# A relational graph convolution: 172 spare columns at the end of a ring of sums, and copies one part behind the matrix engine

## The chip, the core and the metric

The kernel runs on one core of a Trainium2 chip. A core has a matrix engine (TensorE, PE in the profile; its weight loads are PEld), a vector engine (VectorE, DVE), an activation engine (ScalarE, ACT), GpSimd (POOL), a synchronisation engine that issues transfers (SyncE, SP), and 16 DMA engines that all transfers share. Each engine runs its own instructions in order and waits for others by semaphores. SBUF is the on-chip memory with 128 partitions; PSUM holds what TensorE writes. The metric is the device time of one launch in microseconds (us), the median of several runs.

## What is computed

Two layers of a relational graph convolution with 12,500 nodes, 128 features, 200,000 edges sorted by destination, and 10 relations; then a residual and a layer norm. An edge's relation is the argmax of ten of its attributes.

```
def _rgcn_layer(x, src, dst, edge_type, w_rel, root, bias):
    seg = dst * NUM_REL + edge_type
    sums = segment_sum(x[src], seg)
    cnt  = segment_sum(ones, seg)
    mean = (sums / maximum(cnt, 1)[:, None]).reshape(N, NUM_REL, -1)
    return einsum('nrd,rdo->no', mean, w_rel) + x @ root + bias

h   = relu(_rgcn_layer(x, src, dst, edge_type, w_rel1, root1, b1))
out = layernorm(x + _rgcn_layer(h, src, dst, edge_type, w_rel2, root2, b2))
```

## The kernel before

**Tiles and parts.** The edges are cut into 1,563 tiles of 128. `STEP` is 8: on average a tile moves on by 8 destination nodes. `OFF` is 80: a tile's first node lies within 80 of where the average puts it (the kernel clamps it, and falls back to a slow path if an input breaks the bound). Four tiles make a *part* (`QB`); layer 1 is a loop over parts `p`.

**What a part does** (`layer_1`). POOL gathers the rows of the tile's sources into a buffer `g` (`gathered`, L801), one DMA per tile: first from `x`, later from `XH`, which holds rows of `x` beside rows of the first layer's result for nodes that are finished. DVE makes a 0/1 table `oh` that places each edge at (relation, node in the window) (`ones`, L813), and ACT scales it by 1 / count (`weighted`, L807). TensorE multiplies both into `zp` in PSUM (L1038). DVE adds `zp` to the sums `cc` (`sum_into`, L837). From tile 177 on, each tile gives two products, one for layer 1's sums (`cc[:, 0]`) and one for the share of layer 2's sums that can already be known (`cc[:, 1]`).

The order is written out by hand: in the loop's turn `p`, tables are made for part p + 2, scaled for p + 1, rows gathered and multiplied for p, and sums added for p - 2. A list of due times (`todo`) holds the rest; an entry due at `t + n * u` runs `n` parts after its block was finished. `g` has six buffers of eight rows, of which four (`NEAR`), one part each, serve the tiles from 177 on; `zp` has four banks, two per part.

**The ring.** `cc` holds, for each of two layers and ten relations, `RW` columns of nodes: 1,024 (`RN`) and a few behind. Node n has column n mod 1,024, so the ring comes round every 1,024 nodes, that is every 128 tiles; I call that a *lap*. A tile writes 12 columns (`WN`) from its first node's column, which is read at run time from a row `b_r` (DMA at L1049, loaded into DVE's registers at L822, a row per 128 tiles). A tile just in front of a lap's end may so write beyond column 1,023. When the first block of a lap is finished, `folded` adds those columns to the beginning of the ring and clears them:

```
s, e = cc[:, ls, :, :w], cc[:, ls, :, RN:RN + w]
nc.vector.tensor_tensor(s, s, e, op=ALU.add)      # L785
nc.vector.memset(e, 0.0)                          # L786
```

Since the column is known only at run time, each addition declares the lowest and highest column that its tile could have (`offsets`), and the waits are made from that. A tile whose possible nodes lie on both sides of a multiple of 1,024 declares columns 0 to 1,023.

**Blocks.** A *block* is 256 nodes (128 near the end; 52 in all). When all tiles that can reach it are summed, `finish(k, t)` runs: `projected` multiplies its sums by ten relation matrices and the root (L794, L796); ACT adds the bias (`rows_copied`, L717); TensorE transposes the result (`rows_out`, L918), ACT copies it (`rows_kept`, L925), and SP stores it to `XH` (L670) and, not transposed, to `hT` (L930). `projected_rows` multiplies the result by layer 2's ten matrices in three groups per 128 nodes: a product into the one PSUM tile `yb` (L906), ACT's copy to `ys` (L907), SP's store to the table `YD`. `cleared` (ACT, L767) sets the block's columns to zero for the next lap. Gathers may use a block's rows in `XH` from seven parts (`READY`) after it was finished, for blocks 3 to 43.

**Layer 2** goes over the edges again: those that could not be taken in layer 1 are brought together in lists on the chip (`brought_together`, `listed`), and their rows gathered from `YD`. It works in the same memory as the ring (`every` is `cc` as one row per partition): the sums `acc2` begin at column `FIRST`, lists and tables lie below.

Of the kernel before, what the change touches and what calls it, by code (L numbers as in the profile page):

```python
# [39 lines left out]
CT = 128  # L40
YB = 512
RN = 2 * YB
RW = RN + WMAX
RT = 11
REACH = 560
SIGMAS = 4.25
# [10 lines left out]
LOW = 1 << 13  # L57
TOPN = (1 << 14) - 1
OFF = 80
W = 128  # L60
GT = 125
EPS = 1e-5
# [4 lines left out]
def rgcn_resnorm_kernel(ctx: ExitStack, tc: tile.TileContext, x, src, dst, attr, w_rel1, root1, b1,  # L67
# [289 lines left out]
    def places():  # L357
        off = keep.tile([NCH, CT], F32, name="off")
        early(0, nc.vector.tensor_tensor(off, b_i, even, op=ALU.subtract))
        b_f = keep.tile([NCH, CT], F32, name="b_f")  # L360
        lows = keep.tile([NCH, CT], F32, name="lows")
        early(0, nc.vector.memset(lows, 0.0))
        for size in (BN, P):
            for k in range(NBLK - 1):
                if done_after(k) < NT and starts[k + 1] - starts[k] == size:
                    early(0, nc.vector.scalar_tensor_tensor(lows, even, STEP * done_after(k) - 0.5, lows,
                                                            op0=ALU.is_gt, op1=ALU.add))
            if size == BN:
                early(0, nc.vector.tensor_scalar(lows, lows, float(BN // P), None, op0=ALU.mult))
        early(0, nc.vector.tensor_scalar(lows, lows, float(P), None, op0=ALU.mult))  # L370
        early(0, nc.vector.tensor_scalar(b_f, off, float(OFF), -float(OFF), op0=ALU.min, op1=ALU.max))
        early(0, nc.vector.tensor_tensor(b_f, b_f, even, op=ALU.add))
        early(0, nc.vector.tensor_tensor(b_f, b_f, lows, op=ALU.max))
        early(0, nc.vector.tensor_tensor(lows, b_i, lows, op=ALU.is_lt))
        early(0, nc.vector.tensor_scalar(b_i, b_f, 0.0, float(N - 1), op0=ALU.max, op1=ALU.min))
        early(0, nc.vector.tensor_scalar(b_r, b_i, RN - 1, None, op0=ALU.bitwise_and))
        nc.vector.tensor_tensor(off, off, off, op=ALU.mult)
        nc.vector.tensor_scalar(off, off, float(OFF) ** 2 + 0.5, None, op0=ALU.is_gt)
        nc.vector.tensor_tensor(off, off, lows, op=ALU.max)
        worst = keep.tile([NCH, 1], F32, name="worst")  # L380
        nc.vector.tensor_reduce(worst, off, axis=AX.X, op=ALU.max)
        nc.vector.tensor_tensor(fl[:NCH], fl[:NCH], worst, op=ALU.max)
# [397 lines left out]
    def folded(ls, k, w):  # L780

        if block(k)[0] % RN or not k:
            return
# [33 lines left out]
    def offsets(row, t0, n, limits, ring=True):  # L817

        lims = [limits(t0 + j) for j in range(n)]
        if ring:  # L820
            lims = [(lo % RN, hi % RN) if lo // RN == hi // RN else (0, RN - 1) for lo, hi in lims]
        vals = nc.values_load_multi_w_load_instructions(  # L822
            row, engines=[DVE], min_val=min(a for a, _ in lims), max_val=max(b for _, b in lims),
            skip_runtime_bounds_check_because="clamped to these nodes on the chip")[1]
        return [nc.s_assert_within(v, a, b, skip_runtime_bounds_check_because="clamped to these nodes on the chip")
                for v, (a, b) in zip(vals, lims)]
# [50 lines left out]
    def layer_1():  # L877
# [6 lines left out]
        def finish(k, t):  # L884
# [4 lines left out]
                xbs[k] = rows_in(k)  # L889
                fTs[k] = features_in(k, 0, xbs[k])  # L890
            u = QB if t < NT else 0
            folded(ALL, k, WN)
            o = block(k)[0] % RN
            po = [projected(k, 0, cc[:, 0, :, o:o + block(k)[1]], rsb[0], fTs[k])]
            both = has_sums(k)
# [5 lines left out]
                fin_a[k] = shifted(a, k, 0)  # L901

            def projected_rows(b, h, r):
                a, ys = fin_a[k], next_of("ys", staged)
                m = min(HB, NREL - r) * C
                nc.tensor.matmul(yb[:h, :m], a[:, b * P:b * P + h], wsb[1][:, r:r + m // C, :], start=True, stop=True)  # L906
                nc.scalar.activation(ys[:h, :m], yb[:h, :m], AF.Copy)  # L907
# [25 lines left out]
            todo.at(t + u, rows_copied)  # L933
            if k <= K1:
                todo.at(t + 2 * u, rows_out)
                todo.at(t + 2 * u, rows_kept)
            else:
                hbs.pop(k, None)
            todo.at(t + 2 * u, features_kept)
            for j, (b, h, r) in enumerate(groups):  # L940
                todo.at(t + (2 + j if k <= K1 else 1 + j) * u, lambda _, b=b, h=h, r=r: projected_rows(b, h, r))
# [12 lines left out]
            if k + 1 < NBLK - 1:  # L954
                def fetch(t):
                    xbs[k + 1] = rows_in(k + 1)

                def turn(t):
                    n0, n, subs = block(k + 1)
                    pt = ps_f.tile([P, YB], F32, name="pf")  # L960
                    for i, h in subs:
                        nc.tensor.transpose(pt[:, i * P:i * P + h], xbs[k + 1][:h, i, :], ident[:h, :h])
# [10 lines left out]
                todo.at(t + (w + 1) * u, turned_kept)  # L973

        fin_a = {}
        yb = ps_z.tile([P, YB], F32, name="yb")
# [151 lines left out]
    def brought_together(ready, first):  # L1128
# [23 lines left out]
        assert at <= FIRST  # L1152
        yield 1
        nc.vector.memset(below, 1.0)
        nc.vector.tensor_scalar(below[:, :P], columns, place, None, op0=ALU.is_ge)
# [125 lines left out]
    def listed(c):  # L1281
# [48 lines left out]
        w = comp.tile([P, P], F32, name="wb")  # L1330
# [19 lines left out]
    def layer_2():  # L1350
# [396 lines left out]
```

## Time and profile before

| | us |
|---|---|
| median of 3 runs | 3,130.71 (3,126.43 to 3,132.64) |
| profiled execution, whole | 3,124.18 |
| profiled execution, first to last instruction (span) | 3,122.4 |
| POOL busy | 2,296.9 (74%) |
| PE busy | 2,227.4 (71%) |
| DVE busy | 1,631.5 (52%) |
| ACT busy | 1,114.4 (36%) |
| first gather of layer 1 starts / last one | 4.08 / 2,006.72 |
| last gather of layer 2 starts | 3,104.05 |

How to read the rows that follow. A row of the timeline has the start in us, the duration, the engine, the line, the operation with what it writes and reads, the count, and in brackets how long the engine had been idle before it and what ended that. A row of the groups has the count, then the busy time in us, the mean duration in ns, and the idle time before, with what ended most of it. `PE zp L1038` as a releaser is TensorE's product of a part. "issue" means that the profile shows nothing that was waited for. A queue's own instructions (`SPq`, `ACTq`) issue transfers.

### The profile page before, as it was taken

What the parts mean: (1) busy time and instruction counts of PE and PEld (TensorE: products, weight loads), DVE (VectorE), ACT (ScalarE), POOL (GpSimd) and SP (SyncE); (2) the same over time, 40 slices, a digit from 0 to 9 for tenths busy, and PEclk for the clock granted to TensorE, in tenths of its full rate; (3) what the DMA queues carried; (4) which work ended last, traced back from release to release, by engine and by line L of the source; (5) the groups of instructions that cost most, each with busy time, mean ns of one, the idle gap of its engine ahead of it and who ended that gap; (6) DMA issues with size and microseconds to landing.
All of it is one profiled execution on the core that took longest, in us unless ns stands there. A gap on an engine that the chain in (4) does not pass through costs nothing. (4 is left out here: it accounts for less than half of the span.)

```text
span 3122.4 us, 42050 instructions
## 1 busy us (share of the span) xinstructions
PE 2227.4 (71%) x11120; PEld 1813.5 (58%) x11120; DVE 1631.5 (52%) x5055; ACT 1114.4 (36%) x3222; POOL 2296.9 (74%) x2437
## 2 busy tenths in 40 slices
PE   2877776868687877778787777754777777767554
PEld 1656655656575666666666566644666666656543
DVE  6664665847474746464656564368642323333332
ACT  3644442534343444444444444331222212221221
POOL 7777776767777777777776777667777777777775
PEclk7789897979888889888898989855777777776555
DMA  6756656656667666666666666542355555554222
GB/s 175 228 159 189 220 170 192 197 184 204 201 188 219 183 219 186 207 197 198 202 192 204 183 188 191 160 109 61 109 161 165 168 158 159 164 166 131 78 69 56
DMA packets 377357, 529.96 MB, mean 170 GB/s; under 512 B 56782, under 2 KB 284501, under 8 KB 377110
## 3 DMA queue, kind: packets, MB, share of 16 engines
q0 software_dynamic: 99776, 249.91, 28.6%
q1 hardware_dynamic: 249111, 264.44, 26.5%
q10 hardware_dynamic: 28223, 12.82, 1.5%
q8 instruction: 93, 1.52, 0.2%
q14 instruction: 154, 1.26, 0.1%
HBM read 373.17 MB, written 160.19 MB: 171 GB/s over the span
## 5 line engine op out<-in xcount | busy, mean ns | idle before, releaser
L801 POOL DMA_INDIRECT g<-XH,idxE x1386 | 1310.8, 946 | 471.7 <-issue 199.8
L1038 PE MATMUL zp<-oh,g 128*128 128x120 f32 x5898 | 958.2, 312 | 455.9 <-DMA g<-XH,idxE 183.8
L1038 PEld LDWEIGHTS zp<-oh,g 128*128 128x128 f32 x5898 | 859.3, 218 | 676.0 <-issue 182.2
L837 DVE TENSOR_TENSOR cc<-cc,zp 128x240 f32 (+1 forms) x1563 | 607.2, 389 | 780.0 <-PE zp L1038 476.5
L801 POOL DMA_INDIRECT g<-YD,idxB x685 | 647.6, 945 | 208.8 <-issue 135.6
L807 ACT ACTIVATE oh<-oh,wE 128x120 f32<-128x120 f32 (+1 forms) x1740 | 517.8, 374 | 86.0 <-DVE oh L813 66.6
L1540 PE MATMUL zy<-oh,g 128*128 128x12 f32 (+22 forms) x1170 | 240.8, 329 | 232.7 <-DMA g<-YD,idxB 145.1
L1540 PEld LDWEIGHTS zy<-oh,g 128*128 128x128 f32 x1170 | 221.8, 264 | 265.5 <-DMA g<-YD,idxB 120.7
L907 ACT ACTIVATE ys<-yb 128x512 f32<-128x512 f32 (+2 forms) x294 | 154.0, 524 | 617.4 <-PE yb L906 609.9
L906 PE MATMUL yb<-w,a 128*128 128x512 f32 (+1 forms) x576 | 306.1, 619 | 1.4 <-ACT ys L907 1.4
L794 PE MATMUL alone<-cc,w 128*128 128x256 f32 (+2 forms) x920 | 295.4, 498 | 1.8 <-DVE cc L1462 1.8
L794 PEld LDWEIGHTS alone<-cc,w 128*128 128x128 f32 x920 | 237.4, 273 | 45.8 <-DVE cc L1462 2.0
L813 DVE TENSOR_TENSOR oh<-bank,keyE 128x480 f32<-128x480 f32 x391 | 253.4, 648 | 0.0
L794 PE MATMUL pf<-cc,w 128*128 128x256 f32 (+2 forms) x1040 | 241.3, 391 | 5.8 <-DVE cc L785 3.1
L767 ACT ACTIVATE cc<-zero 128x1280 f32<-128x1280 f32 (+2 forms) x184 | 224.7, 1225 | 10.1 <-DVE cc L837 4.1
L794 PEld LDWEIGHTS pf<-cc,w 128*128 128x128 f32 x1040 | 202.9, 209 | 36.1 <-DVE cc L837 4.8
L801 POOL DMA_INDIRECT g<-YD,idxE x177 | 169.5, 957 | 71.5 <-issue 37.8
L801 POOL DMA_INDIRECT g<-in_x_dram,idxE x177 | 167.4, 946 | 55.6 <-issue 34.1
L807 ACT ACTIVATE oh<-oh,wB 128x16 f32<-128x16 f32 (+27 forms) x685 | 159.6, 305 | 128.5 <-DVE oh L813 62.4
L751 ACT ACTIVATE rstd<-mv,eps 128x2 f32<-128x2 f32 (+2 forms) x52 | 15.3, 295 | 519.9 <-DVE mv L749 519.8
L1540 PE MATMUL zq<-oh,g 128*128 128x16 f32 (+24 forms) x554 | 107.3, 314 | 100.1 <-DMA g<-YD,idxB 92.9
L1540 PEld LDWEIGHTS zq<-oh,g 128*128 128x128 f32 x554 | 97.3, 242 | 114.4 <-DMA g<-YD,idxB 76.3
(251 smaller groups left out, 1584.6 us busy)
## 6 DMA issues: line engine op xcount, KB each, us to landing
SD<-cc SPq DMA_DIRECT2D x41, 1280.0 KB
cc<-SD SPq DMA_DIRECT2D x41, 1280.0 KB
YD<-ys SPq DMA_DIRECT2D x194, 256.0 KB
m<-in_edge_attr_dram SPq DMA_DIRECT2D x48, 672.0 KB
g<-XH,idxE POOLq DMA_INDIRECT x1386
YD<-ys SPq DMA_DIRECT2D x97, 128.0 KB
XH<-hb SPq DMA_DIRECT2D x44, 256.0 KB
g<-YD,idxB POOLq DMA_INDIRECT x685
```

The costliest lines, as they stand in the source:

```text
L751: nc.scalar.activation(rstd[:p, s], mv[:p, s, 1], AF.Sqrt, bias=eps[:p])
L767: nc.scalar.activation(cc[:, l, h * H:(h + 1) * H, o:o + n], zero[:, None, :n].to_broadcast([P, H, n]), AF.Copy)
L794: nc.tensor.matmul(po[:, :n], wsb[l][:, r, :], sums[:, r], start=(r == 0), stop=(w is None and r == NREL - 1))
L801: nc.gpsimd.indirect_dma_start(out=g[:, j * C:(j + n) * C], out_offset=None, in_=table, in_offset=bass.IndirectOffsetOnAxis(ap=idx, axis=0))
L807: nc.scalar.activation(s, s, AF.Copy, scale=w)
L813: nc.vector.tensor_tensor(o.rearrange("p (t m) -> p t m", m=m), cols[:, None, :m].to_broadcast([P, n, m]), keys[:, :, None].to_broadcast([ ...
L837: nc.vector.tensor_tensor(s, s, z, op=ALU.add)
L906: nc.tensor.matmul(yb[:h, :m], a[:, b * P:b * P + h], wsb[1][:, r:r + m // C, :], start=True, stop=True)
L907: nc.scalar.activation(ys[:h, :m], yb[:h, :m], AF.Copy)
L1038: nc.tensor.matmul(zp[:, o + l * KW:o + (l + 1) * KW], g[:, (slot[j] + l) * C:(slot[j] + l + 1) * C], oh[:, j * KW:(j + 1) * KW], start=Tr ...
L1540: nc.tensor.matmul(zp[:, j * w:(j + 1) * w], g[:, at * C:(at + 1) * C], oh[:, j * w:(j + 1) * w], start=True, stop=True)
```

## The change

The change has three pieces.

1. *More columns.* `EDGE` = 2 x 80 + 12 = 172 columns stand behind the ring's 1,024 where 120 stood. A tile's column is now counted from the lap in which its *earliest* possible node lies, so a tile in front of a lap's end goes on into the columns behind 1,023 and never wraps by itself; `b_r` is worked out so, and `offsets` declares the same range, which no longer spans the ring. `folded` adds and clears 172 columns instead of 12.
2. *Copies one part later.* `projected_rows` no longer copies its own product. It puts the copy and store (`projected_kept`) aside, and the next group's call, one part later, does them first. `rows_kept` is due at `t + 3 * u` instead of `t + 2 * u`.
3. *Room.* The longer ring takes 4,160 bytes more per partition. Layer 2's tiles `h` and `v` move into the ring's memory below `FIRST`, and `wb` uses `tri`'s buffer.

```
+EDGE = 2 * OFF + WN
+RW = RN + EDGE
...
-        early(0, nc.vector.tensor_scalar(b_r, b_i, RN - 1, None, op0=ALU.bitwise_and))
+        early(0, nc.vector.tensor_scalar(b_r, even, -float(OFF), 0.0, op0=ALU.add, op1=ALU.max))
+        lap_of = keep.tile([NCH, CT], I32, name="lap_of")
+        early(0, nc.vector.tensor_scalar(lap_of, b_r, RN - 1, None, op0=ALU.bitwise_and))
+        early(0, nc.vector.tensor_tensor(b_r, lap_of, b_r, op=ALU.subtract))
+        early(0, nc.vector.tensor_tensor(b_r, b_i, b_r, op=ALU.add))
...
-            lims = [(lo % RN, hi % RN) if lo // RN == hi // RN else (0, RN - 1) for lo, hi in lims]
+            laps = [max(0, (t0 + j) * STEP - OFF) // RN * RN for j in range(n)]
+            lims = [(lo - a, hi - a) for (lo, hi), a in zip(lims, laps)]
...
-            folded(ALL, k, WN)
+            folded(ALL, k, EDGE)
...
             def projected_rows(b, h, r):
+                kept_rows()
                 m = min(HB, NREL - r) * C
-                nc.tensor.matmul(yb[:h, :m], a[:, b * P:b * P + h], wsb[1][:, r:r + m // C, :], start=True, stop=True)
+                nc.tensor.matmul(yb[:h, :m], fin_a[k][:, b * P:b * P + h], wsb[1][:, r:r + m // C, :], start=True, stop=True)
+                unkept.append(lambda: projected_kept(b, h, r))
+
+            def projected_kept(b, h, r):
+                ys = next_of("ys", staged)
+                m = min(HB, NREL - r) * C
                 nc.scalar.activation(ys[:h, :m], yb[:h, :m], AF.Copy)
...
-                todo.at(t + 2 * u, rows_kept)
+                todo.at(t + 3 * u, rows_kept)
...
+            todo.at(t + (i + 1) * u, kept_rows)
...
+        def kept_rows(_=None):
+            if unkept:
+                unkept.pop()()
...
-        vs = [comp.tile([P, 2, C], F32, name=f"v{i}") for i in range(1)]
+        vs = [every[:, FIRST - 4 * BN:FIRST - 3 * BN].rearrange("p (t c) -> p t c", c=C)]
...
-        hs = [comp.tile([P, BN], F32, name=f"h{i}") for i in range(3)]
+        hs = [every[:, FIRST - (i + 1) * BN:FIRST - i * BN] for i in range(3)]
```

What this does to the order of instructions, at three places. First DVE's order with its waits, at the first addition in front of the lap at node 5,120 (L837 before, L844 after; `ISA` rows work out the address in registers; L490 and L495 end an argmax, L813 and L818 make a table). Before:

```order
L490 TENSOR_SCALAR ty<-bank 128x32 [waits DVE_49]
L837 ISA
L837 TENSOR_TENSOR cc<-cc,zp_404 128x20x12 [waits DMAHW0_49,DMAHW2_49,PE_49,Activation_49]
L837 ISA
L837 TENSOR_TENSOR cc<-cc,zp_404 128x20x12 [waits DVE_49]
L813 TENSOR_TENSOR oh_93<-bank,keyE 128x480
L837 ISA
L837 TENSOR_TENSOR cc<-cc,zp_401 128x20x12 [waits PE_49,Activation_49]
```

After:

```order
L495 TENSOR_SCALAR ty<-bank 128x32 [waits DVE_49]
L844 ISA
L844 TENSOR_TENSOR cc<-cc,zp_409 128x20x12 [waits PE_49]
L844 ISA
L844 TENSOR_TENSOR cc<-cc,zp_409 128x20x12 [waits DVE_49]
L818 TENSOR_TENSOR oh_93<-bank,keyE 128x480 [waits Activation_49]
L844 ISA
L844 TENSOR_TENSOR cc<-cc,zp_406 128x20x12 [waits DVE_49,PE_49]
```

The instructions stand as they stood; the additions no longer wait for ACT or for transfers, and the table's own wait for ACT (for the scaling of the buffer's last contents) is now written down where it was implied before.

Second DVE's order at a fold, that of the lap that begins at node 5,120 (`cc<-cc` is the addition, the `MEMSET` behind it the clearing; the sizes are partitions x 20 rows x columns). Before:

```order
L837 TENSOR_TENSOR cc<-cc,zp_402 128x20x12
L785 TENSOR_TENSOR cc<-cc 128x20x12
L786 MEMSET cc 128x20x12
L813 TENSOR_TENSOR oh_92<-bank,keyE 128x480
L837 ISA
```

After:

```order
L844 TENSOR_TENSOR cc<-cc,zp_407 128x20x12
L790 TENSOR_TENSOR cc<-cc 128x20x172
L791 MEMSET cc 128x20x172
L818 TENSOR_TENSOR oh_92<-bank,keyE 128x480
L844 ISA
```

Nothing moved; the two instructions have 3,440 elements per partition instead of 240.

Third ACT's order from the finishing of a block on (`hb<-pf` copies the transposed rows, `ys<-yb` a projected group, `cc<-zero` clears, `oh<-oh` scales one part's four tables). Before:

```order
L807 ACTIVATE oh_97<-oh_97,wE 128x120 x4
L925 ACTIVATE hb_6439<-pf 128x2x128
L907 ACTIVATE ys_99<-yb 128x512
L767 ACTIVATE cc<-zero 128x5x256
L807 ACTIVATE oh_98<-oh_98,wE 128x120 x4
L907 ACTIVATE ys_100<-yb 128x512
L767 ACTIVATE cc<-zero 128x5x256
L807 ACTIVATE oh_92<-oh_92,wE 128x120 x4
```

After:

```order
L812 ACTIVATE oh_97<-oh_97,wE 128x120 x4
L772 ACTIVATE cc<-zero 128x5x256
L812 ACTIVATE oh_98<-oh_98,wE 128x120 x4
L937 ACTIVATE hb_6445<-pf 128x2x128
L919 ACTIVATE ys_99<-yb 128x512
L772 ACTIVATE cc<-zero 128x5x256
L812 ACTIVATE oh_92<-oh_92,wE 128x120 x4
```

The copies of rows and of the first group stand behind the next part's scalings, and the first clearing in front of them; of the number of instructions nothing changed here.

More of the change, by code (lines that the diff above doesn't have):

```diff
@@ L42 @@
 RN = 2 * YB
-RW = RN + WMAX
 RT = 11
@@ L820, in offsets @@
         if ring:
-            lims = [(lo % RN, hi % RN) if lo // RN == hi // RN else (0, RN - 1) for lo, hi in lims]
+            laps = [max(0, (t0 + j) * STEP - OFF) // RN * RN for j in range(n)]
+            lims = [(lo - a, hi - a) for (lo, hi), a in zip(lims, laps)]
+            assert all(hi + WN <= RW for _, hi in lims)
         vals = nc.values_load_multi_w_load_instructions(
@@ L903, in projected_rows @@
             def projected_rows(b, h, r):
-                a, ys = fin_a[k], next_of("ys", staged)
+                kept_rows()
                 m = min(HB, NREL - r) * C
-                nc.tensor.matmul(yb[:h, :m], a[:, b * P:b * P + h], wsb[1][:, r:r + m // C, :], start=True, stop=True)
+                nc.tensor.matmul(yb[:h, :m], fin_a[k][:, b * P:b * P + h], wsb[1][:, r:r + m // C, :], start=True, stop=True)
[3 more added lines that the diff above has]
+                m = min(HB, NREL - r) * C
                 nc.scalar.activation(ys[:h, :m], yb[:h, :m], AF.Copy)
@@ L940, in finish @@
             for j, (b, h, r) in enumerate(groups):
-                todo.at(t + (2 + j if k <= K1 else 1 + j) * u, lambda _, b=b, h=h, r=r: projected_rows(b, h, r))
+                i = 2 + j if k <= K1 else 1 + j
+                todo.at(t + i * u, lambda _, b=b, h=h, r=r: projected_rows(b, h, r))
+            todo.at(t + (i + 1) * u, kept_rows)
             if reused:
@@ L973, in finish @@
                 todo.at(t + (w + 1) * u, turned_kept)
+        unkept = []
+        def kept_rows(_=None):
+            if unkept:
+                unkept.pop()()
         fin_a = {}
@@ L1151, in brought_together @@
         tri = comp.tile([P, P], F32, name="tri")
-        assert at <= FIRST
+        assert at <= FIRST - 4 * BN
         yield 1
@@ L1329, in listed @@
         nc.vector.tensor_scalar(li[:p], li[:p], P - 1, None, op0=ALU.bitwise_and)
-        w = comp.tile([P, P], F32, name="wb")
+        w = comp.tile([P, P], F32, name="tri")
         nc.vector.tensor_scalar(w[:p], li[:p], 1.0, None, op0=ALU.max)
```

## The prediction

> **What bounds the kernel now.** I read the page's groups by engine first. POOL is the busiest engine (74%), and everything it does is issuing row gathers:
>
> ```profile
> L801 POOL DMA_INDIRECT g<-XH,idxE x1386 | 1310.8, 946 | 471.7 <-issue 199.8
> L801 POOL DMA_INDIRECT g<-YD,idxB x685 | 647.6, 945 | 208.8 <-issue 135.6
> L801 POOL DMA_INDIRECT g<-YD,idxE x177 | 169.5, 957 | 71.5 <-issue 37.8
> L801 POOL DMA_INDIRECT g<-in_x_dram,idxE x177 | 167.4, 946 | 55.6 <-issue 34.1
> ```
>
> That is 2,425 gathers, 946 ns busy each. The idle time before one is usually 0.30 us, whatever is named as its releaser, as the timeline of POOL below shows. So a gather that nothing holds up comes 1.25 us after the one before it, in both layers: 2,425 x 1.25 = 3,031 us of the 3,122.4. The kernel is a queue of gathers, and a change is worth what it takes from, or adds to, the delays of that queue. Next, POOL's rows around a place where the ring of sums comes round, and those that mark off layer 1 (177 + 1,386 = 1,563 gathers):
>
> ```profile
> 4.08 1.11 POOL L801 DMA_INDIRECT g<-in_x_dram,idxE  x1 [1.92 <-DVE lane L339]
> ...
> 691.14 0.95 POOL L801 DMA_INDIRECT g<-XH,idxE  x1 [0.30 <-issue]
> 696.41 0.94 POOL L801 DMA_INDIRECT g<-XH,idxE  x1 [4.33 <-PE zp L1038]
> ...
> 708.56 0.94 POOL L801 DMA_INDIRECT g<-XH,idxE  x1 [4.44 <-PE zp L1038]
> ...
> 2006.72 0.94 POOL L801 DMA_INDIRECT g<-XH,idxE  x1 [2.09 <-PE zp L1038]
> 2016.54 0.94 POOL L801 DMA_INDIRECT g<-YD,idxE  x1 [8.88 <-PE zp L1038]
> ...
> 2039.24 0.94 POOL L801 DMA_INDIRECT g<-YD,idxE  x1 [9.29 <-DMA h<-hT]
> ```
>
> From the first gather to the 1,563rd are 2,002.64 us; 1,562 steps of 1.25 would be 1,952.5. So layer 1 loses 50.1 us, nearly all of it like the rows at 696.41 and 708.56: POOL waits until TensorE has read a gather buffer. Why TensorE is late there is in DVE's and ACT's timelines at the next such place:
>
> ```profile
> 829.23 0.84 DVE L837 TENSOR_TENSOR cc<-cc,zp 128x240 f32 x2 [5.09 <-ACT cc L767]
> ...
> 833.98 0.85 DVE L837 TENSOR_TENSOR cc<-cc,zp 128x240 f32 x2 [3.33 <-ACT cc L767]
> ...
> 848.40 0.85 DVE L837 TENSOR_TENSOR cc<-cc,zp 128x240 f32 x2 [7.76 <-ACT oh L807]
> ...
> 857.89 0.84 DVE L837 TENSOR_TENSOR cc<-cc,zp 128x240 f32 x2 [5.09 <-ACT cc L767]
> ```
>
> ```profile
> 826.54 0.38 ACT L925 ACTIVATE hb<-pf 128x256 f32<-128x256 f32 x1 [8.13 <-PE pf L918]
> 827.45 0.60 ACT L907 ACTIVATE ys<-yb 128x512 f32<-128x512 f32 x1 [0.53 <-PE yb L906]
> 827.94 1.26 ACT L767 ACTIVATE cc<-zero 128x1280 f32<-128x1280 f32 x1
> ...
> 845.00 0.52 ACTq L1049 DMA_DIRECT2D row<-b_r  x1
> ```
>
> A tile whose nodes lie on both sides of a multiple of 1,024 is declared as if it could touch the whole ring, so its addition waits for ACT's clearing of another block's columns (L767), and that clearing stands behind two copies in which ACT waits for TensorE. DVE stands idle 21 us per lap. (The 7.76 us is another wait, for the row of offsets that ACT issues at 845.00, also behind such a copy.)
>
> **The change, part by part.** The sum is made against the profiled execution: 3,124.18 us, 6.5 below the median of the runs, 3,130.71. I carry differences over to the median.
>
> *The waits at the lap.* In the order of the changed kernel the additions of those tiles wait for TensorE and DVE alone; what cause ACT's clearing was is gone. The wait for the row of offsets stays. As ACT's copies come a part later in its queue, that row's transfer is issued up to a part (4 x 1.25 = 5 us) earlier, so I expect 3 to 8 us of idle DVE per lap where there were 21. POOL first stands still only after all of this has piled up, since it has four parts of near buffers (20 us) ahead of TensorE; a DVE that is 8 us late is covered by them. So the 50.1 us go, but for half a microsecond in single stretched gathers: -49.5.
>
> *The wide fold.* The twelve additions of the ring's end to its beginning (L785) and the clearings behind them (L786) grow from 240 to 3,440 elements per partition.
>
> ```profile
> L584 DVE TENSOR_TENSOR eqb<-bank,kh 128x1344 bf16<-128x1344 f32 x55 | 85.4, 1552 | 0.4
> ...
> L785 DVE TENSOR_TENSOR cc<-cc 128x240 f32<-128x240 f32 x12 | 4.8, 403 | 0.0
> L786 DVE MEMSET cc<- 128x240 f32 x12 | 3.1, 258 | 1.4
> L1154 DVE MEMSET cc<- 128x1408 bf16 x1 | 1.2, 1232 | 0.2 <-issue 0.2
> ```
>
> The addition's slope is (1,552 - 403) / (1,344 - 240) = 1.04 ns an element, so it takes 403 + 3,200 x 1.04 = 3.73 us; the clearing's is 0.834, so 2.93 us. That is 6.0 us more of DVE per fold. As DVE's time it is hidden under the same 20 us of buffers: TensorE's projection, which reads the folded columns, stands two parts of products behind the tile that starts the fold. But one thing is not hidden. The fold adds two SBUF operands. The timeline of POOL beside DVE at three DVE operations that read two:
>
> ```profile
> 892.27 0.40 DVE L785 TENSOR_TENSOR cc<-cc 128x240 f32<-128x240 f32 x1
> 892.42 1.06 POOL L801 DMA_INDIRECT g<-XH,idxE  x1 [0.30 <-PE zp L1038]
> ...
> 2057.77 1.62 DVE L1188 SCALAR_TENSOR_TENSOR cc<-cc 127x1408 f32<-127x1408 int32 x1
> 2057.97 2.25 POOL L801 DMA_INDIRECT g<-YD,idxE  x1 [0.30 <-issue]
> ...
> 2174.88 1.75 DVE L1242 SCALAR_TENSOR_TENSOR cc<-cc 127x1536 f32<-127x1536 int32 x1
> 2175.36 2.08 POOL L801 DMA_INDIRECT g<-YD,idxE  x1 [0.30 <-issue]
> ```
>
> The gather that starts while such an operation runs is stretched until it ends: 2057.77 + 1.62 = 2059.39, and the gather ends at 2060.22; 2176.63, and 2177.44: 0.83 and 0.81 us later, where a free gather takes 0.95. A gather already under way goes on. So a fold of 3.73 us holds POOL from the next gather's start to the fold's end, that is 3.73 less the wait for that start (0 to 1.25 us, 0.62 in the mean): 3.11 us, between 2.49 and 3.73. Nothing wins that back, because POOL has no slack. Eleven folds fall where POOL sets the pace; the twelfth falls where POOL will wait for layer 1's last rows anyway. 11 x 3.11 = +34.2 us (27.4 to 41.1).
>
> The Trainium skill (SBUF — State Buffer, Who interferes with whom) says two things here. A DVE instruction with two SBUF inputs contends with a GpSimd instruction that reads SBUF; the stretched gathers above agree (2.25 us instead of 0.95). It also says that a probe showed `tensor_tensor` not to stall DMAs, which it infers from descriptor generation needing the write interface; by that the fold would cost POOL nothing, which is the first rival below. The trace speaks for the first statement.
>
> *ACT's copies one part later.* No instruction is added. The copy of a projected group now stands in the next part, ahead of the next group's product into the same PSUM tile, so TensorE could wait for ACT; but ACT, which used to stand idle for TensorE there, comes to the copy first and has a part of 5 us for 0.60. I take 0. The transposed rows are copied and stored a part later too, and gathers seven parts behind read them:
>
> ```profile
> 1566.26 0.37 SPq L670 DMA_DIRECT2D XH<-hb  x1
> ...
> 1580.21 0.95 POOL L801 DMA_INDIRECT g<-XH,idxE  x1 [0.30 <-PE pf L962]
> ```
>
> ```profile
> 547.31 0.37 SPq L670 DMA_DIRECT2D XH<-hb  x1
> ...
> 550.33 0.94 POOL L801 DMA_INDIRECT g<-XH,idxE  x1 [1.09 <-DVE reach L453]
> ```
>
> In a quiet stretch 13.95 us lie between issue and the first reader; where DVE was late, 3.02 sufficed. A part later leaves 5 to 6 us: 0. On SP's queue this store now stands behind the store of the features, 0.46 us.
>
> *The end of layer 1.* From 2006.72 to 2039.24, 32.5 us, POOL issues 12 gathers, the last of which needs all of layer 1's rows. What it waits for is DVE's backlog and the chain behind it:
>
> ```profile
> 1992.44 0.94 POOL L801 DMA_INDIRECT g<-XH,idxE  x1 [0.30 <-issue]
> ...
> 2010.85 1.79 DVE L837 TENSOR_TENSOR cc<-cc,zp 128x240 f32 x4 [1.18 <-PE zp L1038]
> ```
>
> ```profile
> 1932.41 0.95 POOL L801 DMA_INDIRECT g<-XH,idxE  x1 [0.30 <-PE zp L1038]
> ...
> 1943.63 0.84 DVE L837 TENSOR_TENSOR cc<-cc,zp 128x240 f32 x2 [0.41 <-PE zp L1038]
> ```
>
> The tile gathered at 1992.44 is added 18.4 us later, the one before the last lap's end 11.2 us later. I take 11 in place of 18.4 (-7.4), and the last fold's 3.3 us longer addition, for which the projection waits (+3.3): -4.1. The ends are 15.0 us for the stretch (twelve steps; -17.5) and 32.5 + 6.0 (+6.0).
>
> *The rest.* Some rows of setup (three DVE operations on 13x128, 0.3 us each; one more clearing of 0.6 us on ACT, twice) lie where gathers are up to 60 us ahead of the sums: 0. Layer 2 keeps its order; its small tiles only move into the ring's memory: 0, and the same 1,083.2 us from 2039.24 to the end.
>
> Sum: -49.5 + 34.2 - 4.1 = -19.4, so 3,130.7 - 19.4 = **3,111 us**. With the ends of the fold's price (7 either way) and +6/-5 for the end of layer 1, this case reaches from 3,099 to 3,125.
>
> **Rivals.**
> 1. *Long additions don't hold POOL.* Then the fold is free: 3,111 - 34 = 3,077. For it: 9 of the 12 short folds stretched no gather. Against it: with 0.40 us in a beat of 1.25 a fold meets a gather's start about one time in three, and both operations above 1.6 us that met one held it to their end. 0.07.
> 2. *The clearing holds POOL as well; slower.* 11 x 2.93 = 32 us more: 3,143. It turns to slower once a clearing costs POOL over 19.4 / 11 = 1.8 us. Against it stands a gather that started within a clearing and kept its length (0.94 before, 0.95 here):
>
> ```profile
> 567.18 0.26 DVE L786 MEMSET cc<- 128x240 f32 x1
> ```
>
> ```profile
> 567.24 0.95 POOL L801 DMA_INDIRECT g<-XH,idxE  x1 [0.30 <-issue]
> ```
>
>    It is one case, of 0.26 us. 0.06.
> 3. *The change doesn't do what it says:* the laps' waits come back in other shape (the row of offsets, stores of sums), and half of the 49.5 stays: about 3,136. For it: new waits for DMAs stand in the order ahead of some additions; against it: they are for stores a lap old. 0.07.
> 4. *The transposed rows come late.* A store that lands over 11 us later than now (13.95 - 3.02) would hold the 41 gathers that first need a new block (blocks 3 to 43); at 1 us each 3,152. ACT would have to be two parts late. 0.03.
>
> **How the numbers follow.** The likeliest case has the remaining 0.77 and gives 3,111. From 3,095 to 3,128 I leave out rivals 1, 2, 3 and 4 in the main: about 0.2. The bound of what can be told from no change, 0.2%, is 6.3 us. Faster by more: most of the likeliest case and rival 1, 0.80. Within: its edge and part of rival 3, 0.09. Slower: rivals 2 and 4 and the rest of 3, 0.11.
>
> **What would show it.** The wide addition should show 3.7 us and its clearing 2.9; POOL should have, in layer 1, no wait for TensorE above 1 us, but eleven gathers of some 3.5 to 4.7 us beside the folds; DVE should wait for ACT's clearing nowhere; the 1,563rd gather should start near 1,991. I am wrong if gathers beside folds keep 0.95 us (then far faster), if they stay stretched past the addition's end, or if POOL's long waits for TensorE remain.

## The result and the profile after

| | us |
|---|---|
| before, 4 runs | median 3,131.68 (3,126.43 to 3,135.64) |
| after, 4 runs | median 3,103.11 (3,102.76 to 3,103.90) |
| ratio | 0.9910, 95% interval 0.9893 to 0.9927 |
| profiled execution, before / after | 3,124.18 / 3,102.92 |

The change makes the kernel 28.6 us faster in the median, 21.3 in the two profiled executions. The forecast was 19.4 faster. Line numbers of the changed kernel are a few higher than before: L806 is the gather, L790 and L791 the fold's addition and clearing, L844 the addition of products, L772 ACT's clearing, L1058 the products.

The page's groups of the changed kernel for the gathers, which were 945 to 957 ns each before:

```profile
L806 POOL DMA_INDIRECT g<-XH,idxE x1386 | 1344.9, 970 | 422.4 <-issue 200.2
...
L806 POOL DMA_INDIRECT g<-YD,idxB x685 | 648.2, 946 | 208.7 <-issue 129.8
...
L806 POOL DMA_INDIRECT g<-YD,idxE x177 | 169.4, 957 | 61.5 <-issue 36.9
L806 POOL DMA_INDIRECT g<-in_x_dram,idxE x177 | 171.0, 966 | 55.6 <-issue 34.7
```

Layer 1's two groups have a higher mean (970 and 966), and the larger one has less idle time ahead of it (422.4 where 471.7 stood). So POOL waits less and is held longer. The list of groups has the two new sizes, and the list of waits (in all, times, the longest) what POOL and DVE now wait for:

```profile
L790 DVE TENSOR_TENSOR cc<-cc 128x3440 f32<-128x3440 f32 x12 | 44.8, 3735 | 0.0
L791 DVE MEMSET cc<- 128x3440 f32 x12 | 35.1, 2925 | 9.4 <-DVE cc L790 9.4
```

```profile
DVE cc L844 <- PE zp L1058: 555.9, 334, 9.6
POOL g L806 <- issue: 401.6, 1318, 0.3
...
POOL g L806 <- PE zp L1058: 149.6, 491, 0.3
...
DVE cc L844 <- issue: 75.4, 14, 12.0
```

POOL's waits for TensorE are all 0.3 us, the usual pause between gathers. DVE's waits for ACT's clearing, 132.3 us before, are gone from the list. What is left at the laps is a wait of 6.1 to 12.0 us in front of each lap's first addition, which needs the row of offsets; every such row was issued 3.4 to 6.5 us before its addition. The list puts six of these twelve waits under "issue" (they are 53 of the 75.4), and names TensorE for the other six, so how much of each is the row stays open. The timeline of POOL and DVE at a fold, and at the end of layer 1:

```profile
381.81 0.95 POOL L806 DMA_INDIRECT g<-XH,idxE  x1 [0.30 <-issue]
383.06 3.79 POOL L806 DMA_INDIRECT g<-XH,idxE  x1 [0.30 <-issue]
387.15 0.95 POOL L806 DMA_INDIRECT g<-XH,idxE  x1 [0.30 <-issue]
...
382.29 3.73 DVE L790 TENSOR_TENSOR cc<-cc 128x3440 f32<-128x3440 f32 x1
386.81 2.92 DVE L791 MEMSET cc<- 128x3440 f32 x1 [0.78 <-DVE cc L790]
...
1995.20 0.95 POOL L806 DMA_INDIRECT g<-XH,idxE  x1 [0.30 <-PE zp L1058]
...
2008.95 0.94 POOL L806 DMA_INDIRECT g<-YD,idxE  x1 [0.30 <-issue]
2017.80 0.94 POOL L806 DMA_INDIRECT g<-YD,idxE  x1 [7.91 <-DMA cc<-hT]
...
2001.20 1.35 DVE L844 TENSOR_TENSOR cc<-cc,zp 128x240 f32 x3 [4.28 <-PE zp L1058]
```

The gather at 381.81 was under way when the addition began and keeps 0.95 us. The next one ends at 386.85, 0.82 us after the addition's end (386.03). The one at 387.15 runs inside the clearing and keeps 0.95.

Since a gather that nothing holds up follows the last by 1.25 us in every kernel run here, each kernel's time can be cut from POOL's timeline into four stretches: 4.0 to 4.2 us to the first gather; from it to the 1,563rd, 1,952.5 us of pace plus a *loss*; from there to the first gather that needs all of layer 1 (*end of layer 1*); and the rest. Of the loss, the part *beside folds* is what gathers that overlap a fold's additions (in e5 its clearings too) last beyond 0.946 us. For all kernels of this study:

| kernel | loss | beside folds | end of layer 1 | rest | median |
|---|---|---|---|---|---|
| before | 50.1 | 0.3 | 32.5 | 1,083.2 | 3,131.7 |
| after | 38.5 | 36.6 | 22.6 | 1,083.3 | 3,103.1 |
| e1: 20 pieces in a row | 20.0 | 19.9 | 23.0 | 1,084.6 | 3,084.3 |
| e2: operand in PSUM | 0.6 | 0.0 | 23.4 | 1,082.2 | 3,065.0 |
| e3: copies later alone | 1.4 | 0.4 | 23.2 | 1,082.6 | 3,065.6 |
| e4: columns alone | 37.5 | 34.2 | 31.4 | 1,082.4 | 3,108.2 |
| e5: 20 pieces between clearings | 17.0 | 16.1 | 26.8 | 1,083.6 | 3,086.1 |
| e6: fold of 120 columns | 24.4 | 23.6 | 22.2 | 1,083.1 | 3,088.6 |
| e7: transposed rows later alone | 62.3 | 0.1 | 36.1 | 1,082.1 | 3,140.9 |
| e8: projected rows later alone | 3.0 | 0.6 | 22.4 | 1,083.6 | 3,067.2 |
| e9: operand in PSUM, four times | 19.4 | 0.1 | 32.5 | 1,084.6 | 3,094.7 |

The stretches are of the profiled executions, the medians of four runs or more, the profiled one among them.

### The profile page after: what moved, and what is told of

It reads as the page before. It is cut to its first block, busy times and chain, and to the rows that moved or that the text cites. A ratio compares the mean times of both kernels' runs of the same rounds, so it can differ in the third digit from the quotient of the medians.

```text
span 3101.1 us, 42083 instructions
## 1 busy us (share of the span) xinstructions
PE 2228.4 (72%) x11120; PEld 1804.3 (58%) x11120; DVE 1703.7 (55%) x5058; ACT 1117.0 (36%) x3224; POOL 2335.1 (75%) x2437
## 4 chain that ended last, share of the span: by engine, by line
PE 20%; DMA 19%; issue 7%; DVE 5%; POOL 2%; DVEq 0%; ACT 0%; SPq 0%; POOLq 0%; ACTq 0%
DMA g<-YD,idxB 10%; DMA g<-XH,idxE 8%; PE alone L799 8%; PE zp L1058 4%; POOL g L806 2%; PE zy L1560 2%; PE yb L913 2%; PE zq L1560 1%; PE pf L799 1%; PE pf L1284 1%; DVE cc L1589 1%; DVE cc L1252 1%; DMA cc<-hT 1%; DVE go L1240 0%; PE pf L1492 0%
## 5 line engine op out<-in xcount | busy, mean ns | idle before, releaser
L806 POOL DMA_INDIRECT g<-XH,idxE x1386 | 1344.9, 970 | 422.4 <-issue 200.2
L1058 PE MATMUL zp<-oh,g 128*128 128x120 f32 x5898 | 959.6, 308 | 432.7 <-DMA g<-XH,idxE 291.0
L1058 PEld LDWEIGHTS zp<-oh,g 128*128 128x128 f32 x5898 | 848.5, 213 | 656.7 <-DMA g<-XH,idxE 211.3
L844 DVE TENSOR_TENSOR cc<-cc,zp 128x240 f32 (+1 forms) x1563 | 607.0, 388 | 682.6 <-PE zp L1058 555.9
L806 POOL DMA_INDIRECT g<-YD,idxB x685 | 648.2, 946 | 208.7 <-issue 129.8
L818 DVE TENSOR_TENSOR oh<-bank,keyE 128x480 f32<-128x480 f32 x391 | 253.2, 648 | 0.0
L772 ACT ACTIVATE cc<-zero 128x1280 f32<-128x1280 f32 (+2 forms) x184 | 224.5, 1224 | 2.4 <-DVE tri L1178 2.4
L806 POOL DMA_INDIRECT g<-YD,idxE x177 | 169.4, 957 | 61.5 <-issue 36.9
L806 POOL DMA_INDIRECT g<-in_x_dram,idxE x177 | 171.0, 966 | 55.6 <-issue 34.7
```

Source lines behind the costliest of these rows:

```text
L772: nc.scalar.activation(cc[:, l, h * H:(h + 1) * H, o:o + n], zero[:, None, :n].to_broadcast([P, H, n]), AF.Copy)
L806: nc.gpsimd.indirect_dma_start(out=g[:, j * C:(j + n) * C], out_offset=None, in_=table, in_offset=bass.IndirectOffsetOnAxis(ap=idx, axis=0))
L818: nc.vector.tensor_tensor(o.rearrange("p (t m) -> p t m", m=m), cols[:, None, :m].to_broadcast([P, n, m]), keys[:, :, None].to_broadcast([ ...
L844: nc.vector.tensor_tensor(s, s, z, op=ALU.add)
L1058: nc.tensor.matmul(zp[:, o + l * KW:o + (l + 1) * KW], g[:, (slot[j] + l) * C:(slot[j] + l + 1) * C], oh[:, j * KW:(j + 1) * KW], start=Tr ...
```

## The experiments

The theory under test: the wide fold holds POOL because its addition has two operands in SBUF, and this gives back most of what the vanished waits at the laps bring. The rivals: length alone holds POOL; and, on the other part, the later copies of ACT bring nothing of their own.

### The fold's addition in 20 pieces (e1)

```
 # after, folded()
-        s, e = cc[:, ls, :, :w], cc[:, ls, :, RN:RN + w]
-        nc.vector.tensor_tensor(s, s, e, op=ALU.add)
-        nc.vector.memset(e, 0.0)
+        for l in range(ls.start, ls.stop):
+            for r in range(NREL):
+                s, e = cc[:, l, r, :w], cc[:, l, r, RN:RN + w]
+                nc.vector.tensor_tensor(s, s, e, op=ALU.add)
+        nc.vector.memset(cc[:, ls, :, RN:RN + w], 0.0)
```

> The changed kernel with the fold's addition cut into 20 pieces of 172 columns (one per layer and relation); the clearing stays one instruction. Theory: what the fold costs is that an addition with two SBUF operands holds up the next gather until it ends. A piece lasts about 0.34 us (0.16 + 172 x 1.04 ns), so a gather that starts beside the 7 us of pieces waits 0.17 us in the mean and five or six do so: about 1 us per fold instead of 3.05, 12 folds: 3,103 - 24 = 3,079 us. No gather is stretched by more than 0.35 us. Rival (what counts is how long DVE is away from the sums): DVE is busy 3 us longer per fold, so no gain, 3,103 or up to 36 us more.

Measured: 3,084.29 us (3,075.49 to 3,088.27), 0.9847 of before (0.9820 to 0.9875). Nearly half of the fold's price is gone, less than expected: seven of twelve folds still hold a gather to their end, which so lasts 3.41 to 4.16 us where the theory allowed no more than 0.35 us of delay, and five hold none. The timeline of DVE and POOL at one that holds:

```profile
378.92 0.95 POOL L808 DMA_INDIRECT g<-XH,idxE  x1 [0.30 <-issue]
378.98 5.04 DVE L792 TENSOR_TENSOR cc<-cc 128x172 f32<-128x172 f32 x20
...
380.17 0.95 POOL L808 DMA_INDIRECT g<-XH,idxE  x1 [0.30 <-issue]
...
381.43 3.41 POOL L808 DMA_INDIRECT g<-XH,idxE  x1 [0.30 <-PE zp L1060]
```

The gather at 380.17 finds its place among the pieces; the one at 381.43 does not, and ends 0.82 us after the last piece, as if the ten pieces left were one addition. So the mechanism is the same, but cutting an addition up is no safe cure: pieces that follow each other without a pause (20 in 5.04 us) can keep a waiting gather out. Why one gather gets in and the next doesn't, these runs don't show.

### The same pieces with a clearing between them (e5)

```
 # e1
                 nc.vector.tensor_tensor(s, s, e, op=ALU.add)
-        nc.vector.memset(cc[:, ls, :, RN:RN + w], 0.0)
+                nc.vector.memset(e, 0.0)
```

> The kernel after, with its wide fold as 20 pairs: an addition of 172 columns, then the clearing of the same 172 columns, and so on; the same work as 20 additions in a row and one clearing. Theory (an addition with two SBUF operands keeps a gather out only while it runs, and 20 additions in a row gave it no gap): the clearings are gaps, so a gather beside the fold loses at most some 0.3 us, layer 1 loses about 3 us in all, and the time is near 3,068. Rival (DVE's next addition gets ahead of a gather that waits, whatever stands between): gathers are held to the end of the last pair, and as the pairs last some 9 us together, the time is 3,100 or more.

Measured: 3,086.14 us (3,085.42 to 3,087.20), 0.9858 (0.9838 to 0.9877): between the theory's figure and the rival's. The timeline of POOL and DVE at one fold:

```profile
1835.73 0.99 POOL L808 DMA_INDIRECT g<-XH,idxE  x1 [0.30 <-PE zp L1060]
1837.02 1.18 POOL L808 DMA_INDIRECT g<-XH,idxE  x1 [0.30 <-issue]
...
1842.95 1.18 POOL L808 DMA_INDIRECT g<-XH,idxE  x1 [0.30 <-issue]
1844.43 0.95 POOL L808 DMA_INDIRECT g<-XH,idxE  x1 [0.30 <-DVE oh L820]
...
1833.59 0.33 DVE L792 TENSOR_TENSOR cc<-cc 128x172 f32<-128x172 f32 x1
1834.02 0.20 DVE L793 MEMSET cc<- 128x172 f32 x1
1834.14 0.27 DVE L792 TENSOR_TENSOR cc<-cc 128x172 f32<-128x172 f32 x1
```

No gather is held to the end: a clearing of 0.20 us is gap enough, as the theory said. What I had wrong is the number of gathers that pay. The twenty pairs last 10.0 us, and nearly every gather in that time waits for the addition in its way: 74 gathers of 1.16 us in the mean in place of 0.95, 16.1 us in all. The last fold, now 10 us long, adds 3.4 us to the end of layer 1 against e2. Spread out or in a row, the twenty pieces take much the same from POOL (16.1 us against 19.9), about half of what the one addition takes (36.6).

### The same addition with one operand in PSUM (e2)

```
 # after, folded(); iotaP[:, 0:1] is a column of zeros in PSUM
-        nc.vector.tensor_tensor(s, s, e, op=ALU.add)
+        nc.vector.tensor_tensor(s, s, iotaP[:, 0:1, None, None].to_broadcast(list(s.shape)), op=ALU.add)
```

> The changed kernel whose fold adds a constant zero read from PSUM in place of the columns behind the ring: the same 3,440 elements, order and waits, one SBUF operand instead of two. It leaves out the adding of those columns, so its sums at the beginning of each lap lack them. Theory (two SBUF operands hold POOL): the addition keeps about 3.7 us and no gather beside it is stretched: 36.6 us less in layer 1, about 3,066 to 3,070 us. Rival (any long DVE operation holds POOL, or the length of the fold on DVE counts): gathers of 3.5 to 4.5 us remain, 3,103.

Measured: 3,065.01 us (3,062.83 to 3,069.00), 0.9795 (0.9773 to 0.9817). From the list of groups:

```profile
L806 POOL DMA_INDIRECT g<-XH,idxE x1386 | 1310.6, 946 | 422.5 <-issue 188.8 <-PE zp L1058 144.4 <-DMA g<-XH,idxE 40.8
...
L790 DVE TENSOR_TENSOR cc<-cc,bank 128x3440 f32<-128x3440 f32 x12 | 44.8, 3731 | 0.0
```

The addition lasts as long as after's (3,731 ns against 3,735), the gathers have their 946 ns again, and beside the folds nothing is lost (36.6 to 0.0 us). So length alone holds nothing. The zero that e2 reads is also a single column read again and again; that this is not what frees the gathers is seen in the kernel before. Its additions of a part's products (0.27 to 0.41 us) read one operand in SBUF and a whole one, `zp`, in PSUM, as here:

```profile
893.47 0.83 DVE L837 TENSOR_TENSOR cc<-cc,zp 128x240 f32 x2
...
893.79 0.94 POOL L801 DMA_INDIRECT g<-XH,idxE  x1 [0.30 <-issue]
```

In that trace 279 gathers start while such an addition has 0.16 us or more to run, and all of them last 0.94 to 0.96 us. Three gathers start so beside the short fold, whose addition has the same 240 elements and two SBUF operands, and all three are stretched. It is the second SBUF operand that holds a gather.

The Trainium skill (SBUF — State Buffer, Who interferes with whom) says that a DVE instruction with at most one SBUF input, outside DVE's two-port modes, does not contend with GpSimd, and that one with two SBUF inputs does where GpSimd reads SBUF. This pair of runs agrees with both statements, 0.0 and 36.6 us. By the other sentence of the Trainium skill there, that a probe did not see `tensor_tensor` stall DMAs (for a reason that it marks as inferred), both kernels would have taken the same time; the measurement decides against it for these gathers.

### A fold between the two sizes (e6)

The kernel before with the copies one part later (e3, below), and its fold 120 columns wide:

```
-            folded(ALL, k, WN)
+            folded(ALL, k, WMAX)
```

> The kernel before with ACT's copies one part later, and its fold 120 columns wide in place of 12 (2,400 elements a partition, 108 of the 120 columns are always zero): a dose between the short fold and the one of 3,440. Theory (the next gather starts 0 to 1.25 us into the addition and ends 0.82 us after it): the addition takes 403 + 2,160 x 1.04 = 2,650 ns, each of twelve gathers loses 2.65 + 0.82 - 0.95 - 0.62 = 1.9 us, 23 us in all, and the time is 3,065.6 + 23 - 1 = 3,088. Rival (only additions past some length hold POOL): 3,066. Rival (a held gather costs the same whatever the addition's length): 3,101.

Measured: 3,088.63 us (3,086.56 to 3,090.30), 0.9865 (0.9845 to 0.9885); 3,088 was expected. The group of the addition, and POOL and DVE at one fold in the timeline:

```profile
L785 DVE TENSOR_TENSOR cc<-cc 128x2400 f32<-128x2400 f32 x12 | 31.8, 2652 | 0.0
```

```profile
1519.38 3.20 POOL L801 DMA_INDIRECT g<-XH,idxE  x1 [0.30 <-PE yb L906]
...
1519.12 2.65 DVE L785 TENSOR_TENSOR cc<-cc 128x2400 f32<-128x2400 f32 x1
```

1519.12 + 2.65 = 1521.77, and the gather ends at 1522.58, 0.81 us later. Twelve gathers lose 23.6 us, 1.97 each (1.9 expected), where after's lose 3.05. The price grows with the addition's length, and the short fold fits too: in before, the three gathers that are stretched beside a fold of 0.40 us end 0.81 or 0.82 us after it.

### Each part of the change alone (e3, e4)

e3 is the kernel before with ACT's copies one part later and nothing else; e4 is after without that part.

```
 # e3 against before (e4 takes the same lines out of after)
+                kept_rows()
...
+                unkept.append(lambda: projected_kept(b, h, r))
...
-                todo.at(t + 2 * u, rows_kept)
+                todo.at(t + 3 * u, rows_kept)
```

> The kernel before with the second piece alone (ACT copies projected and transposed rows one part later); ring, declared ranges and the fold of 240 elements as before. Theory: DVE's waits at the lap were long because the clearings stood behind copies in which ACT waited for TensorE; with the copies later, a clearing is done about 2 us after a part's products at most, DVE's idle time per lap falls from 21 us below the 20 us of gather buffers, POOL stands still nowhere but at the end of layer 1, where additions still wait for a projection and a store: 48 us less, about 3,083. Rival: the declared range over the whole ring is what costs, and the time stays at 3,120 to 3,131.

Measured: 3,065.59 us (3,064.56 to 3,067.12), 0.9795 (0.9774 to 0.9815), better than the 3,083 expected, since the end of layer 1 shrinks as well (32.5 to 23.2 us), and 37.5 us below the whole change. From the list of waits:

```profile
POOL g L801 <- PE zp L1051: 157.4, 515, 0.7
...
DVE cc L837 <- ACT cc L767: 47.0, 20, 5.3
```

The additions at a lap still declare the whole ring, and DVE still waits for ACT's clearing, 47.0 us in place of 132.3. But no wait is long enough to reach POOL: its longest for TensorE is 0.7 us, and the loss is 1.4 us where it was 50.1.

> The changed kernel without the second piece: the longer ring and wide fold, but ACT copies rows in the same part as before. Theory: the additions in front of a lap no longer wait for ACT, so POOL's long waits for TensorE are gone as in the changed kernel, and twelve stretched gathers (36.6 us) stay: 3,103, at most 5 us more for the row of offsets, which is issued later again. Rival (the copies bring a part of the gain): POOL waits for TensorE come back at the laps, 3,110 to 3,125.

Measured: 3,108.16 us (3,107.98 to 3,109.54), 0.9930 (0.9909 to 0.9951). That is the upper end of what the theory had (3,103, at most 5 us more). The columns alone also end the waits at the laps: eleven gathers held beside folds make 34.2 of the 37.5 us. In the list of waits those in front of the laps' first additions ("issue") have grown, and layer 1 ends 8.8 us later than after's (31.4 against 22.6), since the last additions lag more:

```profile
DVE cc L844 <- issue: 172.2, 17, 14.7
...
POOL g L806 <- PE zp L1056: 155.4, 485, 5.8
```

So either part removes the waits, and both together remove them once. The later copies do it for nothing; the columns cost 34 to 37 us of held gathers. The whole change brings 0.9%; its second part alone brings 2.0%, 63.7 us against the 3,129.25 of before in the runs beside it.

### Which of the two copies (e7, e8)

```
 # e7 against before                              # e8: as e3, with this line as before
-   todo.at(t + 2 * u, rows_kept)                     todo.at(t + 2 * u, rows_kept)
+   todo.at(t + 3 * u, rows_kept)
```

> The kernel before with only the copy of transposed rows one part later; the copies of projected rows stay in the part of their products. Theory (ACT's clearing of a block's columns is late because it stands behind any copy that waits for a TensorE operation of the same part, and one such copy is as late as two): the projected rows' copy takes over the wait of some 8 us, DVE still stands idle for the clearing at the laps, and the time is 3,120 to 3,130. Rival (each copy carries a share of the delay): about half of the 64 us of both, 3,097.

> The kernel before with only the copies of projected rows one part later; the transposed rows are copied in the part of their transposes. Theory, as in the run beside it: the transposed rows' copy keeps its wait of some 8 us ahead of the clearing, and the time is 3,115 to 3,130. Rival: half of the 64 us, 3,097.

Measured: e7 3,140.93 us (3,136.99 to 3,148.35), 1.0034 (1.0018 to 1.0050), slower than before, where the theory expected no gain; why it is slower, and not level, stays open. e8 3,067.17 us (3,066.69 to 3,068.79), 0.9797 (0.9777 to 0.9817), all of e3's gain. e8 goes against the theory and its rival alike. ACT's timeline at the same lap, first e7, with the product that the copy reads and the addition that waits for the clearing, then e8 (L907 and L912 are the copies of projected rows, L930 that of transposed ones, L767 the clearing):

```profile
832.57 1.22 PE L906 MATMUL yb<-w,a 128*128 128x512 f32 x2
...
833.88 0.60 ACT L907 ACTIVATE ys<-yb 128x512 f32<-128x512 f32 x1 [11.15 <-issue]
834.38 1.26 ACT L767 ACTIVATE cc<-zero 128x1280 f32<-128x1280 f32 x1
...
835.67 0.84 DVE L837 TENSOR_TENSOR cc<-cc,zp 128x240 f32 x2 [7.28 <-ACT cc L767]
...
838.62 0.60 ACT L907 ACTIVATE ys<-yb 128x512 f32<-128x512 f32 x1 [1.58 <-PE yb L906]
839.12 1.26 ACT L767 ACTIVATE cc<-zero 128x1280 f32<-128x1280 f32 x1
```

```profile
822.41 0.60 ACT L912 ACTIVATE ys<-yb 128x512 f32<-128x512 f32 x1 [1.35 <-PE yb L906]
827.09 1.27 ACT L767 ACTIVATE cc<-zero 128x1280 f32<-128x1280 f32 x1 [4.08 <-DVE cc L837]
...
845.79 0.38 ACT L930 ACTIVATE hb<-pf 128x256 f32<-128x256 f32 x1 [4.25 <-PE pf L923]
846.07 1.26 ACT L767 ACTIVATE cc<-zero 128x1280 f32<-128x1280 f32 x1
```

A block has one copy of transposed rows but six of projected rows, one in each of the parts in which its clearings fall. In e7 each of these clearings still stands behind a copy of the same part's product (the first one shown ends at 833.79, 0.09 us before its copy starts, though the copy's row names "issue"), and that product stands in TensorE's queue behind products that need DVE to empty `zp`, while DVE waits for the clearing: one round of the four engines per part, several parts in a row. In e8 the clearing at 827.09 waits for DVE's own earlier addition and not for the copy ahead of it, which reads an earlier part's product. The first clearing of a block stands behind the transposed rows' copy still, here after 4.25 us. Copies do wait for TensorE in e8 as well, but less where it counts: between 500 and 1,960 us, ACT's wait in the copies right ahead of a clearing that is not its block's first is 1.6 us in the mean, where e7 has 4.4, and DVE's waits for the clearing are 60.5 us in all (5.6 the longest) where e7 has 139.1 (7.3) and before 132.3 (8.0). That the round repeats per part is read from the queues' order; that it hangs on the projected rows' copies is what the two runs show.

### How much of DVE's time is free (e9)

e2 with the addition made four times:

```
+        for _ in range(4):
             nc.vector.tensor_tensor(s, s, iotaP[:, 0:1, None, None].to_broadcast(list(s.shape)), op=ALU.add)
```

> The kernel after with its wide fold's addition made four times over, each adding a zero from PSUM in place of the columns (which leaves out the adding of those columns): 4 x 3.73 + 2.93 = 17.9 us of DVE per fold, none of it with two SBUF operands. It measures how much DVE time per fold the gather buffers hide. Theory (20 us of buffers between POOL and TensorE): a product at the fold stands some 5 us behind its gather in a quiet stretch, so 15 us are free and each of twelve folds costs 0 to 5 us: 3,065 to 3,125, POOL waiting for TensorE beside the folds and no gather stretched. Rival (nothing but the 6.7 us of the wide fold was covered): 12 x 11.2 = 134 us more, 3,199.

Measured: 3,094.71 us (3,094.22 to 3,099.13), 0.9888 (0.9869 to 0.9908), 29.7 above e2. POOL and DVE in the timeline at the first fold, and POOL at the end of layer 1:

```profile
231.81 0.95 POOL L807 DMA_INDIRECT g<-XH,idxE  x1 [0.30 <-issue]
239.75 0.94 POOL L807 DMA_INDIRECT g<-XH,idxE  x1 [6.99 <-PE zp L1059]
...
217.05 15.04 DVE L791 TENSOR_TENSOR cc<-cc,bank 128x3440 f32<-128x3440 f32 x4
232.75 2.92 DVE L792 MEMSET cc<- 128x3440 f32 x1 [0.67 <-issue]
...
2008.57 0.94 POOL L807 DMA_INDIRECT g<-YD,idxE  x1 [17.83 <-DMA cc<-hT]
```

DVE is taken for 18.6 us here, and POOL stands still from some 16 us after the fold began. That happens at the first, third and fourth fold (6.7, 4.4 and 6.7 us); the others cost at most 0.6 us, but for the last, which delays the end of layer 1 by 9.1 us. So the buffers hide after's fold of 6.7 us with room to spare, and the 36.6 us are not a lack of DVE time.

## Why the prediction was right, and where it was not

- **Direction and mechanism: right.** The addition (3.73 forecast, 3.735) and the clearing (2.93, 2.925) have the forecast lengths. The clearing holds nothing (rival 2; 36 gathers start within one, and all last 0.94 to 0.95 us), long additions do hold POOL (rival 1), no transposed row comes late (rival 4), and half of the lap's waits don't come back (rival 3).
- **The waits at the lap, -49.5: -48.2 measured** (the loss beside what the folds took: 38.5 - 36.6 = 1.9 left of 50.1). The reason given was incomplete: I put all of it down to the columns. e3 and e8 show that the copies of projected rows one part later remove the waits by themselves, and e4 that the columns do too.
- **The row of offsets, "3 to 8 us of idle DVE per lap": too low, without cost.** In front of the twelve laps' first additions DVE stood idle for 6.1 to 12.0 us, over 8 us at five of them. It is hidden by the buffers, as the text said of 8 us, and as e9 shows of longer folds that cost nothing.
- **The wide fold, +34.2: +36.6.** Per gather 3.11 was forecast and 3.05 measured (the prediction's own rows, an end 0.82 us behind the addition and a free gather of 0.95, give 3.73 + 0.82 - 0.95 - 0.62 = 2.98). The mis-sized term is the number: twelve folds, since the twelfth came at 1987.83 while POOL was still at its pace; the first eleven make 33.6. That the twelfth falls "where POOL waits anyway" was read from before, where POOL waited there because of the lap; with that wait gone, the twelfth fold counted.
- **ACT's copies one part later, 0: the step that failed.** Added to the columns they bring some 5 us (e4 against after), at the end of layer 1; added to before they bring 64. I priced the copies by what they add and by who might wait for them, and not by what stands behind them in ACT's queue, though the rows that I showed had the clearing there. The forecast of the whole change came out right all the same, because its two parts remove the same waits.
- **The end of layer 1, -4.1: -9.9** (32.5 to 22.6). I took 11 us for the lag of the last additions behind their gathers, plus 3.3 for the last fold. The 1,563rd tile is added 6.95 us behind its gather, fold and all, where it was 15.88: -8.9. The rows I used were of before, where ACT's copies delayed the additions also in front of a lap; e4, without the later copies, has 14.7 us and an end of 31.4. The range was also drawn too narrow: the two ends given for this stretch, -17.5 and +6.0, lie 13.4 below and 10.1 above -4.1, but the sum took 5 and 6, and -9.9 lies outside that.
- **The rest, 0: +0.3** (1,083.15 to 1,083.34, and 0.07 ahead of the first gather).
- **Carrying the difference over to the median.** In the profiled executions the sum is -48.2 + 36.6 - 9.9 + 0.3 = -21.2 (-21.3 by the spans), against -19.4 forecast; the median fell by 28.6. Before's profiled execution lies 7.5 us below the median of its runs, which spread over 9 us, and after's 0.2 below its own, which spread over 1.1. e3 and e8, which don't have the waits either, spread over 2.6 and 2.1 us, e7, which has them, over 11.4. So the waits at the lap seem to vary from run to run, and the profile showed a light case of them; how much of the 7.3 us this is, the runs don't settle (e1 spreads over 12.8 us without these waits, with folds that hold or don't).

## What to carry to other kernels

Before an engine is relieved by more buffer, look at what stands behind each instruction that waits in its queue: moving six copies one part further from the products that they waited for brought 65 us for no added instruction, and moving the seventh alone brought nothing. Where a queue of indirect gathers sets the pace, count DVE's time in operations with two SBUF operands against it (here some 80% of their length, 36.6 of 44.8 us), and give one operand a place in PSUM where it can be had; cutting such an operation up only halves the price. When two parts of a change remove the same wait, price each alone: one may be the whole gain and the other only cost.

## What the runs showed of the hardware that was not expected

Additions with two SBUF operands, one behind the other without a pause, can keep an indirect gather waiting to the end of the row, in seven folds of twelve; one lasted 3.41 us, past ten additions of 0.25. A clearing of 0.20 us between them, which has no SBUF input, is enough for the gather to pass, and each gather then waits some 0.23 us. A held gather ends 0.81 to 0.83 us after the addition that held it, whatever that addition's length (0.40, 2.65, 3.73 us). A gather that had started 0.04 us before an addition (1196.73 against 1196.77 in e6) kept its 942 ns.
